# Sums of squares brought to the nodes by VectorE's block transposes and a trip through DRAM, in place of TensorE's transposes

## The chip, the cores and the metric

The kernel runs on one core of one Trainium2 chip. The metric is the device time of one execution in microseconds. A core has TensorE (PE in the profile, its weight loads PEld), VectorE (DVE), ScalarE (ACT), GpSimd (POOL) and SyncE (SP, which only issues DMA here). Each engine works through its own queue in the order of the program; they wait for each other by semaphores.

## The reference: what is computed

There are 128 graphs of 128 nodes with 512 features each. Two layers follow each other, and each adds its result to its input and normalises.

```python
# layer 0: graph attention, 8 heads of 64 units, then residual and layer norm
feats = einsum('bnf,hfu->bhnu', X, W)
att   = softmax(leaky_relu(e_self + e_neigh) + NEG_BIG * (1 - A))
x     = _layernorm(x + relu(einsum('bhij,bhju->bhiu', att, feats) + b))

# layer 1: two hypergraph convolutions with a layer norm between them
h = relu(hypergraph_conv(x, adj, W1, b1))      # 1024 hidden features
h = layer_norm(h, gamma, beta)                 # over the 1024, for each node
y = hypergraph_conv(h, adj, W2, b2)
x = _layernorm(x + (y + x))
```

The change concerns the `layer_norm` of `h`. For each node it needs the mean and the mean square of 1024 hidden values. In the kernel `h` lies with hidden features across the 128 partitions and the nodes along the free dimension (8 blocks of 128 features). So the mean square of a node is a sum over partitions, and it is wanted with the nodes on the partitions, as one number per partition, for the scaling of `y`.

## The kernel before

The kernel takes the graphs in 64 pairs and runs as a hand-made pipeline: each step has a lag in periods and a time within a period, and all steps of all pairs are sorted by `(p + lag) * T + time`. This sorted order is the order of the instructions in every engine's queue; the times do nothing else.

The squares and their sums over the 8 blocks, on ScalarE and GpSimd:

```python
    def square(p, s, g, q):
        ...
        nc.scalar.activation(
            s["sq"][:, g, q * KH // 2:(q + 1) * KH // 2, :], hid(s, g, q), AF.Square,
            scale=DH ** -0.5,
        )
    ...
    def squares(p, s, g, level):

        t = s["sq"][:, g]
        n = KH >> (level + 1)
        nc.gpsimd.tensor_tensor(t[:, :n, :], t[:, :n, :], t[:, n:2 * n, :], op=ALU.add)

    for g in range(2):
        for level in range(3):
            at(3, ((17.0, 17.1, 17.2), (26.0, 27.3, 28.0))[g][level], squares, g, level)
```

After that `sq[:, g, 0, :]` holds 128 partial sums for each of 128 nodes. Two transposes on TensorE bring the nodes to the partitions, VectorE sums the 128 columns, and GpSimd makes the factor `rs` from the variance; `y_scale` uses it:

```python
    @step(3, 34.8, until=LAST)
    def sum_squares(p, s):
        s["pm"] = bank(f"pm_{p}")
        for g in range(2):
            nc.tensor.transpose(s["pm"][:, g * N:(g + 1) * N], s["sq"][:, g, 0, :], ident)

    @step(3, 30.62, until=LAST)
    def h_means(p, s):
        ...   # squares of the means, on GpSimd

    @step(3, 36.0, until=LAST)
    def h_rstd(p, s):
        ve = small.tile([P, 2], F32, tag="ve", name=f"veh_{p}")
        nc.vector.tensor_reduce(
            ve, s["pm"][:, :2 * N].rearrange("p (g f) -> p g f", g=2), AX.X, ALU.add
        )
        nc.gpsimd.tensor_tensor(ve, ve, s["m2"], op=ALU.subtract)
        nc.gpsimd.tensor_scalar(ve, ve, 0.0, EPS, op0=ALU.max, op1=ALU.add)
        s["rs", "h"] = small.tile([P, 2], F32, tag="rs", name=f"rsh_{p}")
        nc.gpsimd.tensor_tensor(s["rs", "h"], ve, mhalf, op=ALU.pow)

    def y_scale(p, s, g):
        t = s["y2"][:, g, :, :QU]
        nc.vector.scalar_tensor_tensor(
            t, t, s["rs", "h"][:, g:g + 1], bw_bc.rearrange("p (j c) -> p j c", j=2),
            op0=ALU.mult, op1=ALU.add,
        )

    at(4, 0.6, y_scale, 1, until=LAST)
    at(4, 1.3, y_scale, 0, until=LAST)
    ...
    at(4, 10.9, output, 0, until=LAST)
    at(4, 11.8, output, 1, until=LAST)
```

Steps of other pairs that stand in the queues around these, by time within the period (the lag differs):

```python
    at(2, 27.9, attended, 1)                        # VectorE: y <- pav
    at(3, 30.6, y_sum, 0, 0, 0, "Y", until=LAST)    # VectorE: y2 <- py + pyY
    at(0, 30.65, x_transpose, 1, since=2)           # VectorE
    at(2, 30.7, residual, 1)                        # VectorE: y <- max(y, 0) + x, moments
    at(2, 30.8, rstds, "a")                         # VectorE vea, then GpSimd rsa
    @step(2, 33.12) first_shift                     # ScalarE: sh <- rsa
    at(2, 33.13, first_output, 0)                   # ScalarE: y, also 33.14
    # leaky(0, 0) and (0, 1) at (1, 33.2) and (1, 35.0): ScalarE, eight L592
    at(3, 37.2, y_sum, 1, 0, None, "X", until=LAST) # ScalarE: L874
    at(3, 0.0, propagate, 0)                        # TensorE: pz <- R, y; also 0.9
    at(3, 1.1, z_evict, 0)                          # ScalarE: zT <- pz; also 2.0
    # z_sums at 2.7, 3.4, 4.1, 4.8: GpSimd, zS <- zT;  x_sums from 6.1: GpSimd
    # hidden products at 2.0 (phX <- zT), 3.8, 5.6, 7.35, 9.1, 12.65, 14.4: TensorE
    # h_sum at 5.9, 11.8, 16.4: VectorE;  largest at 2.1 and 7.3: VectorE
    # feature products from 16.2: TensorE (pf);  attend 0 at 20.65: TensorE (pav <- eT)
```

A PSUM bank is a tile of one pool with eight buffers, handed out in turn:

```python
    def bank(name):
        return psum.tile([P, HALF], F32, tag="bank", name=name)
```

Of the kernel before, what the change touches and what calls it, by code (L numbers as in the profile page):

```python
# [8 lines left out]
F32 = mybir.dt.float32  # L9
AF = mybir.ActivationFunctionType  # L10
ALU = mybir.AluOpType
AX = mybir.AxisListType
# [8 lines left out]
def kernel(  # L21
# [45 lines left out]
    nc = tc.nc  # L67
    G, N, F = x.shape
    P = 128
# [10 lines left out]
    B = 32  # L80
    NB = P // B

    const = ctx.enter_context(tc.tile_pool(name="const", bufs=1))
    work = ctx.enter_context(tc.tile_pool(name="work", bufs=1))
    small = ctx.enter_context(tc.tile_pool(name="small", bufs=4))
    dram = ctx.enter_context(tc.tile_pool(name="dram", bufs=3, space=bass.MemoryType.DRAM))
    psum = ctx.enter_context(tc.tile_pool(name="psum", bufs=8, space=bass.MemoryType.PSUM))

    def bank(name):
        return psum.tile([P, HALF], F32, tag="bank", name=name)  # L90
# [109 lines left out]
    for i in range(2):  # L200
        t = const.tile([P, 2, H, UW + 1], F32, name=f"ft{i}")
        nc.gpsimd.memset(t[:, :, :, UW:], 1.0)
        fts.append(t)
    dn = const.tile([P, B], F32, name="dn")
    nc.gpsimd.memset(dn, 0.0)

    def second_sums(engine, w, b12, some=slice(0, 4)):

        b11, b21, b22, t4, t1, t2, t3 = (w[i] for i in range(7))
        for dst, in0, in1 in ((t1, b12, b11), (t2, b22, t1), (t3, b22, b12), (t4, b21, t2))[some]:  # L210
            engine.tensor_tensor(dst, in0, in1, op=ALU.subtract)
# [86 lines left out]
    LAST = PAIRS - 1  # L298
    steps = []

    def step(lag, time, since=0, until=PAIRS):

        def keep(fn):
            steps.append((lag, time, fn.__name__, range(since, until), fn, ()))
            return fn
        return keep

    def at(lag, time, fn, *args, since=0, until=PAIRS):
        steps.append((lag, time, fn.__name__, range(since, until), fn, args))
# [170 lines left out]
    def feature(s, i, to, start):  # L480
# [4 lines left out]
          feature, FW, since=2)  # L485
# [375 lines left out]
    def weigh(s, i, to, start):  # L861
# [3 lines left out]
          QU, 1, until=LAST)  # L865
# [14 lines left out]
    at(4, 0.1, y_sum, 0, 1, 1, "W", until=LAST)  # L880
    at(3, 37.2, y_sum, 1, 0, None, "X", until=LAST)

    @step(3, 34.8, until=LAST)
    def sum_squares(p, s):
        s["pm"] = bank(f"pm_{p}")
        for g in range(2):
            nc.tensor.transpose(s["pm"][:, g * N:(g + 1) * N], s["sq"][:, g, 0, :], ident)  # L887

    @step(3, 30.62, until=LAST)
    def h_means(p, s):  # L890
# [2 lines left out]
        for g, m in enumerate((s["y2"][:, 0, 0, QU:], s["py", 1][:, QU:QU + 1])):  # L893
            nc.gpsimd.tensor_tensor(s["m2"][:, g:g + 1], m, m, op=ALU.mult)

    @step(3, 36.0, until=LAST)
    def h_rstd(p, s):
        ve = small.tile([P, 2], F32, tag="ve", name=f"veh_{p}")
        nc.vector.tensor_reduce(
            ve, s["pm"][:, :2 * N].rearrange("p (g f) -> p g f", g=2), AX.X, ALU.add  # L900
        )
        nc.gpsimd.tensor_tensor(ve, ve, s["m2"], op=ALU.subtract)
        nc.gpsimd.tensor_scalar(ve, ve, 0.0, EPS, op0=ALU.max, op1=ALU.add)
        s["rs", "h"] = small.tile([P, 2], F32, tag="rs", name=f"rsh_{p}")
        nc.gpsimd.tensor_tensor(s["rs", "h"], ve, mhalf, op=ALU.pow)  # L905
# [5 lines left out]
            op0=ALU.mult, op1=ALU.add,  # L911
        )

    at(4, 0.6, y_scale, 1, until=LAST)
    at(4, 1.3, y_scale, 0, until=LAST)

    def output(p, s, g):
        s["pq", g] = bank(f"pq_{p}_{g}")
# [178 lines left out]
    for p in range(PAIRS):  # L1097
        if p > 1:
            todo.append(({2: 79.5, 3: 143.1}.get(p, p * T), load, (p,)))
            todo.append((16.2 if p == 2 else p * T + 19.0, load_blocks, (p,)))  # L1100
            todo.append((p * T + (28.5 if p == 2 else 20.5), load_edges, (p,)))
        for lag, time, name, pairs, fn, args in steps:
            if p not in pairs:
                continue
            if p == 0 and lag == 2 and time < 8.5:
                time *= 0.2
            if p == LAST:

                time = {
                    ("attend", 0): 24.25, ("attended", 0): 25.5, ("add_bias", 0): 25.6,  # L1110
                    ("attend", 1): 25.95, ("attended", 1): 26.0, ("add_bias", 1): 26.1,
                    ("residual", 1): 26.3, ("rstds", "a"): 26.4,
                }.get((name,) + args[:1], time)
            if p == LAST - 1:
                time = {
                    ("product", 2): 24.22 if (lag, time) > (3, 20.0) else time,
                    ("product", 5): 29.5 if (lag, time) > (3, 20.0) else time,
                    ("squares", 0): 26.5, ("squares", 1): 26.6, ("h_sums", 2): 22.3,
                    ("sum_squares",): 43.0, ("h_rstd",): 43.2, ("y_scale", 1): 5.8, ("y_scale", 0): 5.9,
                }.get((name,) + args[:1], time)  # L1120
            time += (p + lag) * T
            todo.append((
                first.get((name, p) + args, first.get((name, p), time)), run, (fn, p, args)
            ))
# [46 lines left out]
```

## Time and profile before

| | |
|---|---|
| time | 2528.1 us, median of 3 runs (2527.55 to 2528.61) |
| span of the profiled execution | 2525.1 us |
| TensorE busy | 2498.3 us, 99% |
| TensorE weight loads busy | 2270.5 us, 90% |
| VectorE busy | 1920.5 us, 76% |
| GpSimd busy | 1789.9 us, 71% |
| ScalarE busy | 1539.4 us, 61% |
| DMA | 343.76 MB, mean 136 GB/s |
| granted TensorE clock | 0.998 of full speed |

Busy time of an engine is the time covered by its instructions. Instructions of one engine overlap at their ends in this profile, so the start of the next one says better than the length when an engine was free again. A row of the groups gives line, engine, operation, output and inputs by the names in the program, shapes and count, then busy us and mean ns of one, then the engine's idle us before these instructions and what ended it. A row of the timeline gives start, length and group, and in brackets the idle time ahead of it and what ended that. A row of the chain gives the start, length and line of a piece of the chain of work that ended last; its times stand 0.17 us behind those of the timeline for the same piece.

### The profile page before, as it was taken

The page shows a single profiled execution, that of the slowest core. Times are in us where ns is not written, and L with a number is a line of the kernel's source. Part 1 is how long each engine was busy: PE and PEld are TensorE (multiplying, and loading weights), DVE is VectorE, ACT ScalarE, POOL GpSimd, SP SyncE. Part 2 cuts the span into 40 slices and gives each one's busy share as a digit, 9 for nine tenths or more (in the row PEclk, how much of TensorE's full clock was granted, in tenths as well). Part 3 has the DMA queues.
Part 4 walks back from the last instruction along what each step waited for, and adds up shares of the span by engine and source line. Part 5 has one row for each costly group of instructions (what it writes and reads, how often), then busy time and mean ns, then how long its engine had stood idle before and what let it go on. Part 6 is the DMA issues. An engine that isn't in the chain of part 4 may idle for free.

```text
span 2525.1 us, 48492 instructions
## 1 busy us (share of the span) xinstructions
PE 2498.3 (99%) x16349; PEld 2270.5 (90%) x16349; DVE 1920.5 (76%) x4332; ACT 1539.4 (61%) x4481; POOL 1789.9 (71%) x2058
## 2 busy tenths in 40 slices
PE   7999999999999999999999999999999999999998
PEld 5899999999999999999999999999899999999997
DVE  7877777777777777777777777777777777777765
ACT  4565665665756656657557566566575665665753
POOL 5767767776777677767766776777677767777774
PEclk9999999999999999999999999999999999999999
DMA  6544445444444454454454444444544544445431
GB/s 187 137 133 140 137 136 147 136 126 148 132 134 143 135 143 137 130 151 133 127 150 133 136 140 139 143 136 125 153 131 130 145 137 140 137 130 152 135 109 52
DMA packets 420840, 343.76 MB, mean 136 GB/s; under 512 B 141272, under 2 KB 370160, under 8 KB 420592
## 3 DMA queue, kind: packets, MB, share of 16 engines
q1 hardware_dynamic: 417120, 336.19, 45.5%
q10 hardware_dynamic: 3472, 4.47, 0.5%
q8 instruction: 131, 2.15, 0.3%
q14 instruction: 117, 0.96, 0.1%
HBM read 238.83 MB, written 101.71 MB: 135 GB/s over the span
## 4 chain that ended last, share of the span: by engine, by line
PE 97%; DVE 1%; DMA 1%; POOL 0%; issue 0%; ACT 0%; SPq 0%; POOLq 0%; DVEq 0%; ACTq 0%
PE phX L792 18%; PE pyX L473 17%; PE phW L792 9%; PE pfX L473 9%; PE pav L662 9%; PE pyW L473 8%; PE phY L792 4%; PE pz L757 4%; PE pq L919 4%; PE pfW L473 4%; PE pyY L473 4%; PE pfY L473 2%; PE pd L429 1%; PE pf L510 1%; PE pm L887 1%; PE py L962 0%
## 5 line engine op out<-in xcount | busy, mean ns | idle before, releaser
L329 ACT COPY py<-pyX 128x257 f32<-128x257 f32 x189 | 70.6, 374 | 539.4 <-PE pyX L473 510.6
L792 PEld LDWEIGHTS phX<-zS,w_sb 128*128 128x128 f32 x3072 | 363.1, 192 | 33.0 <-issue 31.6
L792 PE MATMUL phX<-zS,w_sb 128*128 128x128 f32 x3072 | 374.4, 275 | 2.4 <-POOL xS L455 1.2
L845 POOL TENSOR_TENSOR sq<-sq 128x512 f32<-128x512 f32 (+2 forms) x384 | 343.3, 894 | 20.3 <-ACT sq L833 0.3
L576 POOL TENSOR_TENSOR nb<-nb,neg 128x512 f32<-128x512 f32 x256 | 318.3, 1276 | 7.6 <-DMA nb<-rd 7.6
L592 ACT ACTIVATE nb<-nb,ft 128x128 f32<-128x128 f32 x1020 | 317.3, 389 | 7.5 <-POOL nb L576 7.5
L598 DVE TENSOR_REDUCE nm<-nb 128x4 f32<-128x512 f32 x256 | 174.5, 682 | 187.1 <-ACT nb L592 127.1
L606 ACT ACTIVATE nb<-nb,nm 128x128 f32<-128x128 f32 x1024 | 313.4, 392 | 0.4 <-DVE nm L598 0.4
L709 POOL TENSOR_TENSOR rso<-veo,mhalf 128x2 f32<-128x2 f32 x63 | 44.1, 700 | 372.9 <-DVE veo L707 372.9
L662 PEld LDWEIGHTS pav<-ft,eT 128*128 128x128 f32 x2048 | 248.3, 192 | 8.4 <-DVE eT L639 0.8
L662 PE MATMUL pav<-ft,eT 128*128 128x65 f32 x2048 | 242.6, 272 | 0.0
L473 PE MATMUL pyX<-w_sb,hS 128*128 128x257 f32 x1008 | 242.5, 382 | 0.0
L822 ACT ACTIVATE h<-h,vecs 128x128 f32<-128x128 f32 x768 | 239.6, 393 | 2.2 <-DVE h L807 2.2
L473 PE MATMUL pyX<-w_sb,h 128*128 128x257 f32 x1008 | 239.5, 380 | 0.5 <-ACT py L329 0.5
L473 PE MATMUL pyW<-w_sb,hS 128*128 128x256 f32 x1008 | 238.6, 379 | 0.2 <-DVE y L876 0.2
L473 PEld LDWEIGHTS pyW<-w_sb,hS 128*128 128x128 f32 x1008 | 190.8, 189 | 27.7 <-DVE y L876 0.6
L686 POOL TENSOR_TENSOR y<-y,b_bc 128x512 f32<-128x512 f32 x128 | 162.6, 1271 | 71.8 <-DVE y L677 71.8
L473 PEld LDWEIGHTS pyX<-w_sb,h 128*128 128x128 f32 x1008 | 186.5, 190 | 25.4 <-ACT py L329 0.9
L473 PEld LDWEIGHTS pyX<-w_sb,hS 128*128 128x128 f32 x1008 | 186.2, 190 | 24.2
L909 DVE SCALAR_TENSOR_TENSOR y<-y,rsh,bw_bc 128x512 f32<-128x512 f32 x126 | 148.5, 1217 | 52.9 <-POOL rsh L905 52.9
L627 DVE STREAM_TRANSPOSE eT<-eb 128x512 f32<-128x512 f32 x252 | 163.0, 683 | 1.5 <-DMA eb<-ed 1.3
L833 ACT ACTIVATE sq<-h 128x512 f32<-128x512 f32 x256 | 160.7, 628 | 2.1
(167 smaller groups left out, 5644.9 us busy)
## 6 DMA issues: line engine op xcount, KB each, us to landing
nb<-rd SPq DMA_DIRECT2D x127, 512.0 KB, 6.6
ed<-nb SPq DMA_DIRECT2D x126, 512.0 KB, 2.6
eb<-ed SPq DMA_DIRECT2D x504, 128.0 KB, 2.9
x<-in_x_dram SPq DMA_DIRECT2D x64, 512.0 KB, 9.4
out_dram<-o SPq DMA_DIRECT2D x63, 512.0 KB, 2.8
xb<-in_x_dram SPq DMA_DIRECT2D x248, 128.0 KB, 3.1
a<-in_adj_dram SPq DMA_DIRECT2D x64, 128.0 KB, 8.2
w<-in_adj_dram SPq DMA_DIRECT2D x128, 64.0 KB, 7.5
```

Source lines behind the costliest of these rows:

```text
L473: nc.tensor.matmul(to[:, :n], lhs[:, k, :], rhs[:, k, :n], start=bool(start) and k == 0, stop=(k == nk - 1), skip_group_check=True,)
L576: nc.gpsimd.tensor_tensor(t, t, neg[:, :, None, :].to_broadcast([P, NB, HH, B]), op=ALU.add)
L592: nc.scalar.activation(t, t, AF.Prelu, bias=s["ft"][:, g, h, 0:1], alpha=SLOPE)
L598: nc.vector.tensor_reduce(s["nm"][:, g, hs], scores(p, s, g, hs).rearrange("p b h j -> p h b j"), AX.XY, ALU.max, negate=True,)
L606: nc.scalar.activation(t, t, AF.Exp, bias=s["nm"][:, g, h:h + 1])
L627: nc.vector.transpose(s["eT"][:, g, hs, :].rearrange("p h (b i) -> p h b i", b=NB), s["eb", g][:, :, hs, :].rearrange("p b h j -> p h b j"),)
L662: nc.tensor.matmul(t[:, h * (U + 1):(h + 1) * (U + 1)], s["eT"][:, g, q * HH + h, :], s["ft"][:, g, q * HH + h, 2:], start=True, stop=True,)
L686: nc.gpsimd.tensor_tensor(s["y"][:, g, :], s["y"][:, g, :], b0_bc, op=ALU.add)
L792: nc.tensor.matmul(to[:, m * N:(m + 1) * N], w[:, k, m * P:(m + 1) * P], rhs[:, k, :], start=bool(start) and m == 0 and k == 0, stop=(k == ...
L822: nc.scalar.activation(dst[:, k, :], src[:, k, :], AF.Relu, bias=b1_sb[:, c:c + 1])
L833: nc.scalar.activation(s["sq"][:, g, q * KH // 2:(q + 1) * KH // 2, :], hid(s, g, q), AF.Square, scale=DH ** -0.5,)
L845: nc.gpsimd.tensor_tensor(t[:, :n, :], t[:, :n, :], t[:, n:2 * n, :], op=ALU.add)
```

## The change

For pairs 0 to 61 (`until=LAST - 1`, with `LAST = 63`) the transposes on TensorE are left out. VectorE transposes the 32x32 blocks of `sq`, sums each block's 32 columns, and gathers the result in a small tile `sums_in`, which it transposes by blocks again. Each group of 32 partitions then holds the sums over its own 32 partial sums, for all nodes. They are written to DRAM (`sd`) and read back so that the four groups' sums for the same node come to the same group of partitions (`sums_out`); another block transpose and a reduction over the four make `ve`. GpSimd's part, `h_rstd`, and `y_scale` are moved to later places in the queues. Pair 62 keeps the transposes at the place it had; pair 63 has its own code, unchanged. The purpose is to take the transposes, which are no part of the mathematics, and their PSUM bank off TensorE.

```diff
--- before.py
+++ after.py
@@ -203,6 +203,9 @@
         fts.append(t)
     dn = const.tile([P, B], F32, name="dn")
     nc.gpsimd.memset(dn, 0.0)
+    sums_in, sums_out = (const.tile([P, B], F32, name=n) for n in ("sums_in", "sums_out"))
+    for t in (sums_in, sums_out):
+        nc.gpsimd.memset(t, 0.0)
 
     def second_sums(engine, w, b12, some=slice(0, 4)):
 
@@ -880,11 +883,53 @@
     at(4, 0.1, y_sum, 0, 1, 1, "W", until=LAST)
     at(3, 37.2, y_sum, 1, 0, None, "X", until=LAST)
 
-    @step(3, 34.8, until=LAST)
+
+
+
+
+    @step(3, 30.3, until=LAST - 1)
+    def sum_blocks(p, s):
+
+        t = s["sq"][:, :, 1, :].rearrange("p g (c f) -> p g c f", c=NB)
+        nc.vector.transpose(t, s["sq"][:, :, 0, :].rearrange("p g (c n) -> p g c n", c=NB))
+        nc.vector.tensor_reduce(
+            sums_in[:, :2 * NB].rearrange("p (c g) -> p g c", g=2), t, AX.X, ALU.add
+        )
+        s["sr"] = work.tile([P, B], F32, tag="sr", name=f"sr_{p}")
+        nc.vector.transpose(s["sr"], sums_in)
+
+    @step(3, 30.32, until=LAST - 1)
+    def write_sums(p, s):
+        s["sd"] = dram.tile([NB, B, B], F32, tag="sd", name=f"sd_{p}")
+        nc.sync.dma_start(s["sd"].rearrange("b q n -> (b q) n"), s["sr"])
+
+    @step(3, 31.5, until=LAST - 1)
+    def read_sums(p, s):
+
+        for c in range(NB):
+            nc.sync.dma_start(
+                sums_out[c * B:c * B + 2 * NB],
+                s["sd"][:, 2 * c:2 * c + 2, :].rearrange("b g n -> b (g n)"),
+            )
+
+    @step(4, 1.0, until=LAST - 1)
+    def sum_rest(p, s):
+        t = work.tile([P, B], F32, tag="so", name=f"so_{p}")
+        nc.vector.transpose(t, sums_out)
+        s["ve"] = small.tile([P, 2], F32, tag="ve", name=f"veh_{p}")
+        nc.vector.tensor_reduce(
+            s["ve"], t[:, :2 * NB].rearrange("p (b g) -> p g b", g=2), AX.X, ALU.add
+        )
+
+    @step(3, 43.0, since=LAST - 1, until=LAST)
     def sum_squares(p, s):
         s["pm"] = bank(f"pm_{p}")
         for g in range(2):
             nc.tensor.transpose(s["pm"][:, g * N:(g + 1) * N], s["sq"][:, g, 0, :], ident)
+        s["ve"] = small.tile([P, 2], F32, tag="ve", name=f"veh_{p}")
+        nc.vector.tensor_reduce(
+            s["ve"], s["pm"][:, :2 * N].rearrange("p (g f) -> p g f", g=2), AX.X, ALU.add
+        )
 
     @step(3, 30.62, until=LAST)
     def h_means(p, s):
@@ -893,12 +938,9 @@
         for g, m in enumerate((s["y2"][:, 0, 0, QU:], s["py", 1][:, QU:QU + 1])):
             nc.gpsimd.tensor_tensor(s["m2"][:, g:g + 1], m, m, op=ALU.mult)
 
-    @step(3, 36.0, until=LAST)
+    @step(4, 5.0, until=LAST)
     def h_rstd(p, s):
-        ve = small.tile([P, 2], F32, tag="ve", name=f"veh_{p}")
-        nc.vector.tensor_reduce(
-            ve, s["pm"][:, :2 * N].rearrange("p (g f) -> p g f", g=2), AX.X, ALU.add
-        )
+        ve = s["ve"]
         nc.gpsimd.tensor_tensor(ve, ve, s["m2"], op=ALU.subtract)
         nc.gpsimd.tensor_scalar(ve, ve, 0.0, EPS, op0=ALU.max, op1=ALU.add)
         s["rs", "h"] = small.tile([P, 2], F32, tag="rs", name=f"rsh_{p}")
@@ -911,8 +953,8 @@
             op0=ALU.mult, op1=ALU.add,
         )
 
-    at(4, 0.6, y_scale, 1, until=LAST)
-    at(4, 1.3, y_scale, 0, until=LAST)
+    at(4, 6.0, y_scale, 1, until=LAST)
+    at(4, 6.05, y_scale, 0, until=LAST)
 
     def output(p, s, g):
         s["pq", g] = bank(f"pq_{p}_{g}")
@@ -1116,7 +1158,7 @@
                     ("product", 2): 24.22 if (lag, time) > (3, 20.0) else time,
                     ("product", 5): 29.5 if (lag, time) > (3, 20.0) else time,
                     ("squares", 0): 26.5, ("squares", 1): 26.6, ("h_sums", 2): 22.3,
-                    ("sum_squares",): 43.0, ("h_rstd",): 43.2, ("y_scale", 1): 5.8, ("y_scale", 0): 5.9,
+                    ("h_rstd",): 4.6, ("y_scale", 1): 5.8, ("y_scale", 0): 5.9,
                 }.get((name,) + args[:1], time)
             time += (p + lag) * T
             todo.append((
```

## The prediction

> **What bounds the kernel now.** I read the page's engine totals first, then the waits of TensorE, then the chain of work over one period in the middle of the run, then the timelines of the engines beside it. The totals and the rows of the operations concerned, from the page and from the groups of instructions (out<-in, count | busy us, mean ns | idle us before, releaser):
>
> ```profile
> PE 2498.3 (99%) x16349; PEld 2270.5 (90%) x16349; DVE 1920.5 (76%) x4332; ACT 1539.4 (61%) x4481; POOL 1789.9 (71%) x2058
> L887 PE MATMUL pm<-ident,sq 128*128 128x128 f32 x126 | 24.1, 273 | 0.0
> L899 DVE TENSOR_REDUCE veh<-pm 128x2 f32<-128x256 f32 x63 | 26.1, 415 | 5.2 <-PE pm L887 5.2
> ```
>
> TensorE looks full, and the transposes to be removed are 126 of its 16349 matmuls. The chain of work in order of time (start, length, what) around them says what they take of TensorE's time:
>
> ```profile
> 1211.89 0.44 PE pd L429 x4
> 1212.34 0.22 PE pm L887 x2
> 1212.56 1.74 PE pyX L473 x8
> ```
>
> So a pair of transposes takes 0.22 us. The same place comes again after 38.66 us (pd at 1211.89, then 1250.56). If TensorE alone set the period, 0.22 us of 38.66 would be the gain. Whether it does must be seen where TensorE takes something from a slower engine soon after. The first such place is phX, which needs zT from ScalarE. ScalarE's timeline (start, length, group) in that stretch, and then TensorE's:
>
> ```profile
> 1211.54 0.20 ACT L725 ACTIVATE nmean<-mva 128x2 f32<-128x2 f32 x1 [0.91 <-DVE mva L702]
> 1212.52 0.48 ACT L727 ACTIVATE sh<-nmean,rsa 128x1 f32<-128x1 f32 x2 [0.78 <-POOL rsa L709]
> 1212.91 1.51 ACT L734 ACTIVATE y<-y,sh,rsa 128x512 f32<-128x512 f32 x2
> 1214.32 2.43 ACT L592 ACTIVATE nb<-nb,ft 128x128 f32<-128x128 f32 x8
> 1216.66 0.35 ACT L874 COPY y<-pyX 128x256 f32<-128x256 f32 x1
> 1216.95 0.58 ACT L769 COPY zT<-pz 128x512 f32<-128x512 f32 x1
> ```
>
> ```profile
> 1215.86 1.95 PE L757 MATMUL pz<-R,y 128*128 128x128 f32 x16
> 1217.64 2.00 PE L792 MATMUL phX<-zT,w_sb 128*128 128x128 f32 x16
> ```
>
> ScalarE runs without a pause from 1212.52 to 1217.53 and hands zT over at 1217.53 (1216.95 + 0.58); phX begins at 1217.64. Then the instructions on zT there (count: shortest/median/longest ns):
>
> ```profile
> L792 PE MATMUL phX<-zT,w_sb x16: 275/275/323, 1217.6 to 1219.4; 128*128 128x128 f32 x16
> ```
>
> One of the 16, the first, takes 323 ns instead of 275. Near the start of the run (53.5 us), where zT had been ready about 1 us before, all sixteen take 275 to 276. So those 0.05 us are a wait: in the steady state phX already stands at the very edge of zT. Near 96 us, where the list of waits has TensorE waiting for zT once (1.7 us), a copy begun at 95.62 ends at 96.20 and phX starts at 96.25, the same hand-over of 0.05.
>
> What does zT hang on? Followed back: the copy waits for its turn on ScalarE; ScalarE has run unbroken since rsa (GpSimd, 1211.79 to 1212.49), which waited for vea (VectorE, 1211.54 to 1211.71), which ends an unbroken VectorE stretch that began with this:
>
> ```profile
> 1208.54 0.42 DVE L876 TENSOR_TENSOR y<-py,pyY 128x257 f32<-128x257 f32 x1 [2.07 <-PE pyY L473]
> ```
>
> The stretch after it is y_sum, a transpose of xT (1.10), the residual (0.65), bn_stats (0.69), bn_aggr, vea. It starts when TensorE has finished pyY. So from pyY's end to phX there are two ways: TensorE's own queue (pyX, pyW, pd, pm, pyX, pyW, pz), and VectorE, GpSimd, ScalarE. Both end at 1217.6. The transposes lie inside the first way only.
>
> How close is the second? The copy of zT also waits for the first half of pz (eight matmuls of 0.11 from 1215.86, the last ending at about 1216.92), so its 1216.95 might be TensorE's doing. ScalarE's own pace without such a gate is seen at 95 us: L874 begins at 95.37 and zT at 95.62, 0.25 later. Here it is 0.29 (1216.66 to 1216.95). The slack of the second way is therefore 0.04 us. This is the figure the whole prediction rests on.
>
> **What the Trainium skill says.** "VectorE: DVE Perf Modes", The three transpose paths: VectorE transposes 32x32 blocks only, not a whole 128x128. The code agrees: a block transpose leaves sums of 32 partial rows on four groups of partitions, and this is why a trip through DRAM is needed. "Trainium Kernel Development and Optimization", Performance Expectations: matmul busy time is a bad metric, because matmuls are pipelined. This trace agrees: a 99% busy TensorE contains the 0.05 us wait above. "GPSIMD Engine Reference", Specifications: GpSimd contends with VectorE instructions that have two SBUF inputs. The trace agrees: y_scale (L909) has a median of 1212 ns beside GpSimd's sums and 747 at the least, and a GpSimd sum of 128x256 takes 0.72 to 0.73 us undisturbed and 1.05 to 1.17 beside y_scale. "DMA: Bandwidth & Descriptors", Queues, rings and completion order: descriptors are consumed in ring order on each DMA engine. No run here tests it alone; dnb's 8.7 us from issue to landing behind nb's 1 MB fits.
>
> **The change, part by part.** It applies to pairs 0 to 61 of 64.
>
> - TensorE loses 62 x 0.22 = 13.6 us and one PSUM bank per period. With 18 banks taken per period in place of 19, phX inherits pyX's bank, released by L874 at 1217.01; that is before zT, so it costs nothing.
> - VectorE loses the reduction from PSUM (0.41). It gains, after `attended`, a transpose of 128x256 (0.45, as L406), a reduction of 128x256 (0.41, as L899), a transpose of 128x32 (0.21 to 0.24, as L354 and L529): about 1.15 with small gaps. They stand where VectorE waits 2.07 us for pyY, and sq is ready at 1205.57 while VectorE is free at 1206.46: from 1206.5 to 1207.65, so y_sum still starts at 1208.54. Later come a transpose and a small reduction, about 0.4, at 1217.85, where VectorE waited 0.85 us for rsh. All of it is hidden.
> - DMA: one write of 16 KB, four reads of 1 KB. The write is issued at about 1207.7 and lands behind dnb (issued 1205.13, plus 8.7: 1213.8), the reads are issued then at about 0.45 each, behind x's 512 KB: estimate 1217 to 1218, against need at 1217.85. VectorE may wait up to 1.5 us there and lose nothing, since its next work waits for ScalarE until about 1219.6. The next loads of a and w are issued some 5 us later; `nodes` needs them at 1226.5 plus a period, with an estimated 3 us to spare.
> - GpSimd: its three small operations for rsh (1.29 us together) go from before zS to behind it. zS can begin at about 1218.2 instead of 1218.65 and end at about 1221.2; rsh comes at about 1222.4.
> - VectorE's y_scale (2.3 for two) goes from 1218.72 to about 1222.5, behind h_sum. `largest` moves from 1223.80 to 1224.7, h_sum for the second half from 1227.81 to about 1228.6. ScalarE's relu waits for that, and its run ends about 0.7 later, before the copy of pf at 1233.01, ahead of which it idled 0.88. eT, due at TensorE at 1236.14, comes some 0.2 later, at about 1235.5. No new wait of TensorE follows, but what is left is only 0.2 to 0.6 us.
>
> Sum per period: TensorE reaches phX 0.22 earlier and finds zT only 0.04 earlier. Gain 0.04; the other 0.18 becomes waiting. 62 x 0.04 = 2.5 us. Against it, in the first periods VectorE has no idle time ahead of y_sum (it runs unbroken from 84.50 to 90.40), so the 1.15 us of the new work go straight onto the chain once: about 1.2. So 2528.1 - 2.5 + 1.2 = 2526.8, say 2527.
>
> **Rivals.** (1) TensorE's throughput is the bound and the whole 0.22 comes through: 2528.1 - 13.6 = 2514.5. For it: 99% busy and a chain that the profile draws along TensorE almost alone. Against it: the 323 ns, and the 0.04. (2) The moved y_scale makes VectorE late, and a later hand-over (copy of pf, or eT) stalls TensorE by 0.1 to 0.5 us a period: plus 6 to 31 us, 2533 to 2558. For it: only 0.2 to 0.6 us left there. Against it: skip (L745) may run at 686 ns, its median, once GpSimd is done, which gives time back. (3) The DRAM trip lands late and VectorE waits beyond 1219.6: what it loses goes on to y_scale, and 1 us more would be about 0.5 us a period, 2555. For it: the queue is full just then. Against it: it is a few KB with about 9 us from issue to use.
>
> **Range and chances.** The centre follows from the 0.04. The low end, 2518, lets two thirds of rival 1 through; the high end, 2537, lets about 0.15 us a period of rivals 2 or 3 through. Over 2% (50 us) faster would need four times what the removed work takes: 0.01. Over 2% slower needs 0.8 us a period: 0.03. Within 2%: 0.96.
>
> **What would show it.** Right: the period stays at 38.6 us; the TensorE-side waits of phX for zT (L769), almost absent now, become a row of about 62 x 0.2 = 12 us, counting TensorE or its weight load; TensorE's busy time falls by about as much; ScalarE's zT begins 0.25 after L874 in every period; y_sum still waits for pyY, by about 0.9 us instead of 2.07; y_scale starts near 1222.5 of that period. Wrong: a period of 38.44 (rival 1), which would mean that the way through VectorE and ScalarE was not at its limit; waits of TensorE for pf or eT (rival 2); VectorE waiting for the DMA of the sums for more than 1.5 us (rival 3).

## The result and the profile after

The changed kernel takes 2532.5 us (median of 6, 2531.6 to 2534.3) against 2527.8 us (median of 6, 2527.1 to 2528.6): a ratio of 1.0019, with a 95% interval of 1.0006 to 1.0032. It is slower by some 5 us; 2527 was predicted, in a range of 2518 to 2537. The totals of the page after:

```profile
PE 2500.8 (99%) x16225; PEld 2253.8 (89%) x16225; DVE 2014.2 (80%) x4580; ACT 1539.8 (61%) x4481; POOL 1794.0 (71%) x2060
```

TensorE has 124 matmuls less and is busy 2.5 us longer. Its busy time doesn't show waits as short as those that follow. The chain of work in order of time (start, length, piece), from the middle of the run:

```profile
1215.55 0.44 PE pd L432 x4
1215.99 1.73 PE pyX L476 x8
...
1221.24 2.02 PE phX L795 x16
...
1240.14 1.81 PE pav L665 x16
```

In the kernel before, the same two groups were:

```profile
1217.80 1.83 PE phX L792 x16
...
1236.53 1.73 PE pav L662 x16
```

pm, which stood between pd and pyX with 0.22 us, is gone. The first phX group, which took 1.83 us, takes 2.02, and the first pav group, 1.73 before, takes 1.81. So 0.22 us were removed and 0.19 + 0.08 = 0.27 came back as waiting. From one first pz to the next is 38.71 us in most periods, 38.66 to 38.67 before. ScalarE's timeline (start, length, group) and, from the answer on zT, the instructions that use it (ns: shortest/median/longest) show where phX's wait ends:

```profile
1220.33 0.35 ACT L877 COPY y<-pyX 128x256 f32<-128x256 f32 x1
1220.58 1.28 ACT L772 COPY zT<-pz 128x512 f32<-128x512 f32 x2
```

```profile
L795 PE MATMUL phX<-zT,w_sb x16: 275/275/377, 1221.2 to 1223.0; 128*128 128x128 f32 x16
```

zT begins 0.25 us after L877, ScalarE's own pace, where it was 0.29 before. phX's first matmul takes 377 ns; it was 323. Both hold in all 60 periods from the third to the 62nd. In the list of waits of TensorE's weight loads (us in total, times, longest) there are now these two rows:

```profile
PEld pav L665 <- issue: 12.2, 54, 0.3
PEld phX L795 <- ACT zT L772: 8.4, 25, 1.8
```

Before, the list had no such row for pav and one wait of 1.9 us for zT. It leaves short waits out: it counts 25 for zT, where phX waits in all 60. "issue" says that the profile shows nothing that pav waited for there; that it is eT, which pav's weight loads read, is shown below by the kernel that makes eT earlier. VectorE's timeline of the same period (in brackets the idle time before, and what ended it):

```profile
1210.92 0.43 DVE L894 STREAM_TRANSPOSE sq<-sq 128x256 f32<-128x256 f32 x1
...
1212.19 0.42 DVE L879 TENSOR_TENSOR y<-py,pyY 128x257 f32<-128x257 f32 x1
...
1223.76 0.21 DVE L918 STREAM_TRANSPOSE so<-sums_out 128x32 f32<-128x32 f32 x1 [2.23 <-DMA sums_out<-sd]
...
1226.14 2.35 DVE L951 SCALAR_TENSOR_TENSOR y<-y,rsh,bw_bc 128x512 f32<-128x512 f32 x2 [0.30 <-POOL rsh L947]
...
1239.14 1.29 DVE L630 STREAM_TRANSPOSE eT<-eb 128x512 f32<-128x512 f32 x2
```

The new sums stand ahead of y_sum (L879), which now follows them with no idle time to speak of, where VectorE had waited 2.07 us for pyY. The wait for the DMA of the sums, 2.23 us here, is the longest of the whole run. The answer on `sums_out` counts these waits (us, times):

```profile
  DMA sums_out<-sd: 13.4, 17
```

So in most of the 62 periods the sums are there when VectorE comes to them. y_scale (L951) has moved behind, and what follows, down to eT, is later.

Over the profiled executions the loss adds up as follows. From the first pz to the last it is 2435.95 us before and 2441.31 after, 5.36 more. The first two periods are longer by 0.84 together (44.00 + 40.29 against 42.88 + 40.57); five periods of 39.02 to 39.18 exceed 38.71 by 2.1 in all; the other periods give 60 x 0.04 = 2.4.

### The profile page after: what moved, and what is told of

The parts are those of the page before. It is cut to its first block, busy times and chain, and to the rows that moved or that the text cites. A ratio compares the mean times of both kernels' runs of the same rounds, so it can differ in the third digit from the quotient of the medians.

```text
span 2531.1 us, 48862 instructions
## 1 busy us (share of the span) xinstructions
PE 2500.8 (99%) x16225; PEld 2253.8 (89%) x16225; DVE 2014.2 (80%) x4580; ACT 1539.8 (61%) x4481; POOL 1794.0 (71%) x2060
## 4 chain that ended last, share of the span: by engine, by line
PE 92%; DVE 2%; DMA 2%; ACT 1%; issue 1%; SPq 1%; POOL 1%; DVEq 0%; POOLq 0%; ACTq 0%
PE phX L795 18%; PE pyX L476 16%; PE phW L795 9%; PE pfX L476 8%; PE pav L665 8%; PE pyW L476 8%; PE phY L795 4%; PE pq L961 4%; PE pz L760 4%; PE pfW L476 4%; PE pyY L476 4%; PE pfY L476 2%; PE pd L432 1%; PE pf L513 1%; DMA xb<-in_x_dram 1%
## 5 line engine op out<-in xcount | busy, mean ns | idle before, releaser
L609 ACT ACTIVATE nb<-nb,nm 128x128 f32<-128x128 f32 x1024 | 319.4, 391 | 4.6 <-DVE nm L601 0.4
L825 ACT ACTIVATE h<-h,vecs 128x128 f32<-128x128 f32 x768 | 245.0, 392 | 53.6 <-DVE h L810 53.6
L373 DVE STREAM_TRANSPOSE xT<-xb 128x512 f32<-128x512 f32 x124 | 138.0, 1114 | 57.1 <-DMA xb<-in_x_dram 57.1
L951 DVE SCALAR_TENSOR_TENSOR y<-y,rsh,bw_bc 128x512 f32<-128x512 f32 x126 | 148.6, 1218 | 19.0 <-POOL rsh L947 18.5
```

What stands on the lines that cost most here:

```text
L609: nc.scalar.activation(t, t, AF.Exp, bias=s["nm"][:, g, h:h + 1])
L825: nc.scalar.activation(dst[:, k, :], src[:, k, :], AF.Relu, bias=b1_sb[:, c:c + 1])
L951: nc.vector.scalar_tensor_tensor(t, t, s["rs", "h"][:, g:g + 1], bw_bc.rearrange("p (j c) -> p j c", j=2), op0=ALU.mult, op1=ALU.add,)
```

## The experiments

The theory: between pyY and phX two ways run side by side, TensorE's queue and the way over VectorE, GpSimd and ScalarE to zT; the second had 0.04 us to spare. Rival 1 of the prediction: TensorE's throughput is the bound, and the change then loses its gain by its own new work. Rival 2: the moved y_scale makes eT late. Rival 3: the trip through DRAM is what costs. All ratios are to the kernel before, with their 95% intervals; the period is the usual distance from pz to pz.

| kernel | us | ratio | period |
|---|---|---|---|
| before | 2528.5 | 1 | 38.67 |
| without transposes | 2525.4 | 0.9987 (0.9981 to 0.9994) | 38.63 |
| transposes twice | 2541.8 | 1.0053 (1.0038 to 1.0068) | 38.89 |
| before, order of copies | 2528.3 | 1.0000 (0.9991 to 1.0009) | 38.67 |
| without transposes, order of copies | 2513.8 | 0.9943 (0.9928 to 0.9958) | 38.45 |
| after, order of copies | 2533.4 | 1.0020 (1.0010 to 1.0030) | 38.72 |
| after, skip early | 2526.9 | 0.9995 (0.9986 to 1.0003) | 38.63 |
| after, both | 2515.9 | 0.9952 (0.9937 to 0.9967) | 38.45 |
| after, no trip | 2535.7 | 1.0028 (1.0017 to 1.0039) | 38.72 |
| after, both, pair 0 old | 2514.6 | 0.9946 (0.9931 to 0.9961) | 38.45 |
| after, both, pd behind pz | 2556.9 | 1.0112 (1.0095 to 1.0129) | 39.13 |

### What the transposes alone are worth

The kernel before with the transposes left out; VectorE reduces `sq` as it lies, so the variance is a wrong one:

```diff
-    @step(3, 34.8, until=LAST)
-    def sum_squares(p, s):
-        ...   # the two nc.tensor.transpose
-            ve, s["pm"][:, :2 * N].rearrange("p (g f) -> p g f", g=2), AX.X, ALU.add
+            ve, s["sq"][:, :, 0, :], AX.X, ALU.add
```

> The kernel before with the two transposes of each pair left out; VectorE sums sq itself where it summed pm, so the variance used is a wrong one, and nothing else is changed. Theory (the way from pyY over VectorE, GpSimd and ScalarE to zT has only 0.04 us of slack): the period falls from 38.66 to about 38.62, the time by about 2.5 us to 2525, and the first phX matmul waits about 0.2 us for zT. Rival (TensorE's throughput is the bound, and the new work of the change eats the gain elsewhere): period 38.44, time about 2514.

And with each transpose done twice:

```diff
-        for g in range(2):
+        for g in (0, 1, 0, 1):
             nc.tensor.transpose(s["pm"][:, g * N:(g + 1) * N], s["sq"][:, g, 0, :], ident)
```

> The kernel before with both transposes of each pair done twice (same result). Theory: TensorE's own way to phX grows by 0.22 and is then the longer one: period 38.66 + 0.22 = 38.88, time about 2542. Rival (throughput bound): the same. If instead both ways were far from the limit: 2528. Together with the kernel without transposes this shows whether adding 0.22 costs 0.22 while removing 0.22 brings 0.04.

Measured: 38.63 us and 2525.4 without, 38.89 and 2541.8 with twice as many. Adding 0.22 us costs 0.22; removing it brings 0.04. Rival 1, which asked for 2514, falls. ScalarE's timeline and the piece of the chain, without transposes:

```profile
1216.52 0.35 ACT L874 COPY y<-pyX 128x256 f32<-128x256 f32 x1
1216.78 1.30 ACT L769 COPY zT<-pz 128x512 f32<-128x512 f32 x2
```

```profile
1217.45 2.01 PE phX L792 x16
```

Nothing of the new work is in this kernel, and phX takes 2.01 us already, as in the changed kernel. It begins 0.05 us after the end of zT's first copy in every period from the third to the 62nd, so zT is what it waits for, and not the PSUM bank that L874 releases.

### Whether ScalarE's way is the limit

ScalarE's copy of the first half of zT is put ahead of the copy of y, in the kernel before as it is and without transposes. In the latter an unused PSUM bank is taken for each pair, for phX would otherwise get the bank that the copy of y releases.

```diff
-    at(3, 1.1, z_evict, 0)
+    at(3, 0.4, z_evict, 0)
-    at(3, 37.2, y_sum, 1, 0, None, "X", until=LAST)
+    at(4, 0.5, y_sum, 1, 0, None, "X", until=LAST)
+    @step(3, 34.8, until=LAST)          # only with the transposes left out
+    def spare(p, s):
+        bank(f"spare_{p}")
```

> The kernel before with one change of order on ScalarE: the copy of the first half of zT goes ahead of the copy of y (L874). Transposes kept. Theory: zT is then held by pz alone, which it was within 0.04 us already: period 38.66 or at most 0.05 less, time 2525 to 2528. Rival: no change, 2528.

> Both together: transposes left out (a wrong variance is used), the copy of zT ahead of the copy of y, and an unused PSUM bank taken per pair so that the banks go round as before. Theory: ScalarE comes to zT 0.25 us earlier, so the whole 0.22 comes through at phX: period 38.44 to 38.48, time 2514 to 2517; the two edits bring 2.5 and 0 to 2 alone and 11 to 14 together. Rival (throughput bound): the same as the kernel without transposes, 2514, with nothing from the order.

Measured: 2528.3, so the order alone does nothing; 2513.8 with both. The edits bring about 3 and 0 us alone and 14.7 together. This is what two ways of nearly equal length do: shortening one gives almost nothing until the other is shortened too. The chain with both has phX back at its old length, while pm is gone:

```profile
1213.40 1.83 PE phX L792 x16
```

### What the change adds to it

The changed kernel with the order of copies, with `skip` moved ahead of the second reduction of the sums, and with both. VectorE idles there: in the period shown for the DMA, in most periods for ScalarE's nb (1.26 us ahead of the next reduction, the median).

```diff
-    at(3, 9.3, skip, 0)
-    at(3, 9.4, skip, 1)
+    at(3, 0.5, skip, 0)
+    at(3, 0.6, skip, 1)
```

> The changed kernel with the copy of the first half of zT ahead of the copy of y on ScalarE (and an unused PSUM bank per pair, so that the banks go round as in the kernel before). Theory (VectorE is late now by the moved y_scale, and eT is the next limit, anchored on work that does not come earlier with phX): phX no longer waits for zT (1.83 us in place of 2.02), but pav waits more for eT (about 0.25 in place of 0.08); period 38.68 to 38.71, time 2530 to 2532. Rival (the loss is the wait for zT alone): period 38.52, time 2521.

> The changed kernel with VectorE's two skip instructions (L748, 1.7 us) moved from between largest and nodes to before the second reduction of the sums, where VectorE waits 2.2 us for the DMA. Theory: eT comes over 1 us earlier, pav's 0.08 us wait goes, the output and so the loads of xb leave earlier and the rare 0.45 us longer periods go; phX still waits 0.19 for zT. Period 38.62, time 2524 to 2526. Rival (the DRAM trip or its DMA load is what costs): no change, 38.71 and 2532.

> Both edits on the changed kernel. Theory: no limit is left but TensorE: period 38.44 to 38.46, time 2514 to 2518, which beats both kernels; the two edits bring about 1 and 7 alone and 15 together. Rival (the wait for zT alone): 2521 as with the copy order alone. Rival (the trip): 2525 or more.

The chain of the changed kernel with the order of copies, then with skip early, then with both, at phX and at the first pav:

```profile
1220.94 1.83 PE phX L795 x16
...
1239.71 1.97 PE pav L665 x16
```

```profile
1218.83 2.01 PE phX L795 x16
...
1237.73 1.73 PE pav L665 x16
```

```profile
1213.59 1.83 PE phX L795 x16
...
1232.32 1.73 PE pav L665 x16
```

With phX's wait gone, pav waits 0.24 us instead of 0.08: the period is 38.72, no better, and the time 2533.4, a little above the 2530 to 2532 expected. With skip early pav's wait goes and phX's stays: 38.63, and 2526.9, just above the 2524 to 2526 expected. With both, phX and pav take what they took in the kernel before: 38.45, 2515.9. Against the kernel before measured beside them they stand at +4.9 and -1.6 us alone and -12.6 together, the changed kernel at +4.7: the edits bring -0.2 and 6.4 alone and 17.3 together. The changed kernel thus had two limits beside TensorE, zT and eT. The second is the change's own (rival 2), since pav takes 1.73 us in the kernel before without transposes. This version beats both kernels.

### Whether the trip costs

The write of the sums and the four reads are left out; the second reduction sums zeros, so a wrong variance is used:

```diff
-        nc.sync.dma_start(s["sd"].rearrange("b q n -> (b q) n"), s["sr"])
-        for c in range(NB):
-            nc.sync.dma_start(sums_out[c * B:c * B + 2 * NB], ...)
```

> The changed kernel without the trip: the write of the sums to DRAM and the four reads are left out, so the second reduction sums zeros and a wrong variance is used; all VectorE, GpSimd and TensorE work stays. Theory: VectorE's 2.2 us wait for the DMA goes, but y_scale still waits for rsh behind GpSimd's zS, so little changes: period 38.68 to 38.71, time 2530 to 2532. Rival (the trip is the cost): period 38.62 or less, time 2526 or less.

VectorE's timeline then:

```profile
1226.81 2.35 DVE L946 SCALAR_TENSOR_TENSOR y<-y,rsh,bw_bc 128x512 f32<-128x512 f32 x2 [0.31 <-POOL rsh L942]
```

No wait for the sums is left, and y_scale still waits 0.31 us for rsh (0.30 with the trip): the period is 38.72. The changed kernel's own trace agrees: in ordinary periods y_scale begins 6.84 us after pz, whether VectorE waited 2.23 us for the sums before or not at all. The trip is hidden, and rival 3 falls. The time is 7.2 us above that of the kernel before beside it, where the changed kernel is 4.7 above. The profiled executions differ by 1.2 us (2532.4 and 2531.1), with six periods of 39.0 to 39.2 us against five; where the rest of the 2.5 us comes from is open.

### The start of the run, and the last 0.05 us

Pair 0 keeps the transposes, in the version with both edits:

```diff
-    @step(3, 30.3, until=LAST - 1)
+    @step(3, 30.3, since=1, until=LAST - 1)
     def sum_blocks(p, s):
     ...                       # likewise for the other new steps
+    @step(3, 34.8, until=1)
+    def sum_squares_first(p, s):
+        ...                   # the two transposes, the reduction at 36.0
```

> The changed kernel with both edits of order, and pair 0 keeping the transposes on TensorE at their old place (pairs 1 to 61 use the new way). Theory (the one-time loss at the start is the 1.15 us of block transposes and reduction ahead of pair 0's y_sum, where VectorE has no idle time): the distance from the first pz to the second falls from 43.92 to about 42.8, all later periods stay 38.45, time 1.1 us less than with both edits, about 2515. Rival (the loss at the start comes from elsewhere, the loads or y_scale's new place): 43.9 as before.

The first period falls from 43.92 to 43.08 us; 42.8 was expected, 42.88 is the kernel before's. The time falls by 1.3 to 2514.6, about as expected, but the ranges of the two versions overlap (2513.9 to 2515.3 and 2515.0 to 2517.2), so the period is the firmer evidence.

In the other kernel pd goes between pz and phX:

```diff
-    @step(1, 34.7)
+    @step(2, 1.95)
     def propagator(p, s):
     ...
-    @step(1, 35.8)
+    @step(2, 2.15)
     def r_evict(p, s):
```

> The changed kernel with both edits of order, and pd (0.44 us of TensorE) moved from ahead of the last py products to between pz and phX, with its eviction moved behind. Theory (the 0.05 us that phX's first matmul still takes longer is the hand-over pz, copy, phX itself, and not ScalarE's load): phX finds zT ready, 1.78 us in place of 1.83, period 38.40, time about 2513. Rival (the 0.05 us is a cost of starting phX after pz whatever the copy does): 38.45, 2516.

The time is a miss: 2556.9. VectorE's timeline says why, and the answer on zT what became of the question:

```profile
1233.91 0.45 DVE L409 STREAM_TRANSPOSE hT<-ab 128x256 f32<-128x256 f32 x1 [5.20 <-PE pd L432]
```

```profile
L795 PE MATMUL phX<-zT,w_sb x16: 275/275/275, 1233.7 to 1235.4; 128*128 128x128 f32 x16
```

hT is one buffer: the next pair's hT can't be written until pd has read it, and VectorE stands 5.2 us in front of it. The expectation had not followed pd's input, and a version with a second buffer was not run. But phX's first matmul takes 275 ns like the others: the extra 0.05 us was the hand-over from pz over the copy to phX. With the transposes doubled, where ScalarE has 0.22 us more to spare, it is still there:

```profile
L792 PE MATMUL phX<-zT,w_sb x16: 275/275/322, 1225.3 to 1227.1; 128*128 128x128 f32 x16
```

## Why the prediction was right, and where it was wrong

**The range held, the sign did not.** A gain of 1.3 us was worked out and a loss of 4.7 came. 2532.5 lies in the range because the range left room for rivals 2 and 3, up to 0.15 us a period; rival 2 came with 0.08. What was right of the mechanism is the bound, and what failed is the hand-over of eT.

**The bound and the 0.04 us: right.** Removing the transposes gives 0.04 us a period, and phX takes 0.19 us longer. The figure came from ScalarE's pace seen in one early period (0.25 from L874 to zT) against 0.29 in the steady state, and after the change it is 0.25 in each of the 60 periods. One piece of the evidence was read too far: the 323 ns are a wait, but for the hand-over from pz over the copy to phX, which is there with any slack on ScalarE's side, as the doubled transposes show.

**"No new wait of TensorE follows": this step failed.** It said of eT that it "comes some 0.2 later, at about 1235.5" and left 0.2 to 0.6 us. In the kernel before, eT's transposes began 1.81 us before the first pav (1234.56 and 1236.37), now 0.84 (1239.14 and 1239.98). Up to the h_sum of the second half the working was close. Counted from pz's start, y_scale begins after 6.85 us, where 6.86 were predicted (1222.5 less 1215.64, since pz comes 0.22 earlier without the transposes), and h_sum after 13.1, where 13.0 were. But of the 0.8 us by which h_sum was to be later, the prediction let only 0.2 reach eT. The one idle time of VectorE between the two in the timeline before is 0.65 us ahead of the last h_sum, which is about the difference. It was not to spare. The variance of the output (veo), GpSimd's first sum of sq after rso, the first of the two normalisations and eT, in the kernel before and then after:

```profile
1231.30 0.17 DVE L707 TENSOR_SCALAR veo<-mvo 128x2 f32<-128x2 f32 x1
1232.21 1.27 POOL L845 TENSOR_TENSOR sq<-sq 128x512 f32<-128x512 f32 x1
1232.72 1.04 DVE L712 TENSOR_SCALAR o<-o,mvo,rso 128x512 f32<-128x512 f32 x1
1234.56 1.29 DVE L627 STREAM_TRANSPOSE eT<-eb 128x512 f32<-128x512 f32 x2
```

```profile
1235.89 0.17 DVE L710 TENSOR_SCALAR veo<-mvo 128x2 f32<-128x2 f32 x1
1236.80 1.27 POOL L848 TENSOR_TENSOR sq<-sq 128x512 f32<-128x512 f32 x1
1236.87 1.48 DVE L715 TENSOR_SCALAR o<-o,mvo,rso 128x512 f32<-128x512 f32 x1 [0.23 <-POOL rso L712]
```

From veo to eT it is 3.26 us before and 3.25 after. The first normalisation starts 0.51 us into GpSimd's sum before and 0.07 after, and in both it ends 0.28 us after that sum. So the idle time was filled, the normalisation became longer by 0.44 us, and nothing was won: counted from pz's start, veo and eT both come 1.15 us later. With skip moved, both come 0.78 us earlier than that, veo to eT is still 3.26, and pav's wait is gone. This was rival 2 of the prediction, just under the low end of its 0.1 to 0.5 us.

**"All of it is hidden", of the sums ahead of y_sum: half right.** y_sum starts 0.11 us after pyY's end, as before, in all periods but the first, the last and five others. But 0.9 us of idle time was predicted and almost none is left: attended came later. The waits for xb went from 16.0 us in 28 cases to 57.1 in 60, and the residual that follows took 1.42 us in place of 0.86. Where xb is later still, the whole way is. The chain of one of the long periods:

```profile
429.11 3.20 DMA xb<-in_x_dram
...
437.68 0.10 DVE y L879
...
446.10 0.49 ACT zT L772
...
446.64 1.38 PE phX L795 x10
```

It runs from a load of xb through VectorE's sums into y_sum and on to zT. phX waits 0.49 us in this period. The 2.07 us of idle time had been a cushion against late loads, and the change filled it. The other four long periods have the same mark: y_sum begins 0.56 to 0.71 us after pyY's end in these five, where VectorE had waited 1.5 to 1.7 us for xb, and in no other but the first and the last. The kernel without the trip has six long periods and the same six late y_sums, so the trip does not cause them. With both edits, where y_sum waits 0.67 us for pyY again, no period after the second exceeds 38.51:

```profile
1242.99 0.42 DVE L879 TENSOR_TENSOR y<-py,pyY 128x257 f32<-128x257 f32 x1 [0.67 <-PE pyY L476]
```

The load's own lateness leads back to the late normalisations: ahead of it in SyncE's queue stands the write of the output, and the chain of the long period at 446 us comes to the load over that queue from the second normalisation (424.47, 0.96 us). With skip moved, where the normalisations are earlier, the waits for xb fall to 15.4 us in 26 cases. No run changes the order of that queue alone.

**The DRAM trip: right.** The sums were to arrive about when VectorE wants them, 2.2 us after pz's start, and in most periods VectorE takes them at 2.14 to 2.20 without a wait. The 2.23 us at 1223.76, on which the expectations of the runs without the trip and with skip moved rest, is one period's wait, and the only one above the 1.5 named as the sign of rival 3. Even there VectorE waits for rsh afterwards, ahead of y_scale.

**The start: nearly right.** 1.2 us were predicted; the first period lost 1.12, of which 0.28 came back in the second.

**The signs: one was useless.** TensorE's busy time was to fall with the waits and rose by 2.5 us. The row of waits for zT has 8.4 us where 12 were predicted: 62 x 0.19 is 11.8, but the list leaves shorter waits out. The lengths of the groups in the chain were the sign to read. One sum was off: rival 3's 0.5 us over 62 periods are 31 us, so 2558 and not 2555.

So the sum went wrong in its period term, -0.04 us where the trace has +0.04 (62 x 0.08 = 5.0 us), and left out the long periods (2.1 us); the start was 0.4 us too dear. That is 6.7 us by the profiled executions; the medians differ by +4.7 where -1.3 was worked out, 6.0 us.

## What to carry to other kernels

An engine that is 99% busy need not be the only limit: before taking work from it, follow each of its inputs back to a common starting point and compare the two lengths; the gain is at most the difference. Where two ways are within some tens of nanoseconds, only shortening both pays (3 and 0 us alone, 14.7 together). Idle time ahead of a step on such a way is a cushion against late loads, and work that is put there or moved behind it has to be followed to the next hand-over. One engine's idle time is slack for a step only if the step's chain runs over that engine then: 0.65 us of VectorE's idle time were worth nothing here, because the chain to eT ran over GpSimd meanwhile. And one period is not the run: the wait of 2.23 us was the longest of 62.

## What was unexpected of the hardware

VectorE slows down beside GpSimd's sums even with a single large input. The normalisation (128x512, one tensor and two columns of scalars) takes 540 ns at the least, with a median of 950. Beside GpSimd's first sum of sq its end follows the sum's: it comes 0.28 to 0.29 us after the sum's end in each of 58 periods of the kernel before and of the changed one, though the normalisation starts 0.51 us into the sum in the one and 0.07 in the other. Even the smallest operation can wait its turn. In the kernel before, an operation on 128x2 elements started at 91.19 us took 1.27 us while GpSimd added 128x512 (four in 4.95 us from 91.17), and the same operation takes 0.17 in the middle of the run.
